# An attention-and-whitening kernel on one core: weight copies on GpSimd, and an image's last row point prepared in the strict order

## The chip, the cores and the metric

The kernel runs on one core of a Trainium2 chip. The core has five engines that run beside each other: TensorE (matrix multiplication, PE in the profile, with its weight loads as PEld), VectorE (DVE), ScalarE (ACT), GpSimd (POOL) and SyncE (SP, which here only issues DMAs). The metric is the device time of one execution in microseconds. The kernel before was timed in three runs: 761.77, 763.97 and 764.57 us, median 763.97.

## The reference

Input x has 4 images of 256 channels and 64 x 64 pixels, in float32. The first layer computes, for each pixel, 49 attention weights and uses them to average the pixel's dilated neighbourhood:

```python
k = conv(x, w1, 7x7, dilation 2, padding 6) + b1        # 256 -> 128 channels
k = conv(k, w2, 1x1) + b2                               # 128 -> 49
attn = softmax(k, axis=1)
shifts = stack([xp[:, :, 2*u:2*u+64, 2*v:2*v+64] for u in range(7) for v in range(7)])
x = einsum('bkchw,bkhw->bchw', shifts, attn)
```

The second layer whitens the result over the batch: the channels form 4 groups of 64, each group has its mean taken off and its 64 x 64 covariance computed over all images and pixels, five Newton steps give the inverse square root of the covariance, and that matrix is applied to each pixel, followed by a gain and a shift.

## The kernel before, in words

**The convolution.** The two convolutions are merged into one from 256 channels to 49 outputs. Because of the dilation of 2, the image splits into even and odd rows and columns. The 7 x 7 merged convolution is computed by evaluation at points, as in fast convolution: rows and columns each have seven points (0, 1, 2, 3, 4, 5 and INF, where INF is the leading coefficient). For one image and one *row point*, VectorE combines the image's rows (`row_eval`, tiles `rb`), then the columns of that for each column point (`col_ops`, tiles `xh`, through a scratch tile `ct`), TensorE multiplies by the weights of the pair of points (`conv_bank`, tiles `wr`, into the PSUM tiles `cv`), and ScalarE copies the sums to `pv` (line 541). The column points of a row point come in three groups, called banks: points 1, 2, 0, then 3, 4, INF, then 5. Bank 0 has 96 matrix instructions in the profile for a row point with two row taps, bank 1 has 80, and bank 2 has 32; the row point INF has half of each.

**Interpolation.** When a row point's three banks are in `pv`, VectorE turns its column points back into columns (`col_interp`, 22 operations, into the tiles `zz`). When an image has all of its row points, `row_interp` does the same over rows, into the logits `lgx`. At the end of an image this is cut in parts: `row_interp` part 0 follows row point 4, since it needs all row points but 5; row point 5's columns and the rest of the rows follow when its banks come.

**Order of row points.** Image 0 has a start of its own with a partly direct convolution. Image 1 uses the row points 0, 1, 2, 3, 4, 5, images 2 and 3 use INF, 0, 1, 2, 3, 4, 5 (`ROWS`, line 29, so `ROWS[-2]` is row point 4 and `ROWS[-1]` is 5). `conv_step(k, i)` runs bank i of the k-th row point and then prepares bank i of the next one (`prepare`, line 696): its weights, its rows if i is 0, and its columns. The preparation writes `xh` and `wr` tiles of which there is one for each bank, so it has to wait until TensorE has read the previous row point's bank i.

**Weights.** The weights of a pair of points are made once, the first time that a row point is used, and stored to DRAM (`weights`, line 361, store at 429); later images load them (line 375). Making them takes sums and scaled sums on VectorE (through `ct` from image 1 on), for the column points 0 and INF plain copies by ScalarE (lines 405, 406 and 415), and scaling by ScalarE (line 428). Row points 1, 2 and 3 are made for image 0. From image 1 on this happens for row points 0, 4 and 5 of image 1 and for INF of image 2. For 4, 5 and INF the row-combined weights are first brought into `rb[0]` by a DMA on SP's queue (line 384).

**The rest.** Beside an image's convolution runs the attention of the image before it: softmax, the copies of its terms to `zt` (line 906), their way through DRAM (`sd`) and back as a band matrix (`band`, loaded at line 947 and transposed by VectorE at 957), transposed blocks of x (`xb`, TensorE 975, ScalarE 983), the weighted sums y (TensorE 1004, ScalarE 1023), and the moments for the whitening (1036, 1044, 1057). The band tile is loaded again when the y matmuls that read it are done. GpSimd clears tiles and issues the loads of x and the spills of finished images (lines 130 and 1075). After the last image come the remaining sums, the Newton steps and the application.

**What sets the order.** A scheduler in the framework orders each engine's instructions from priorities (the place in the program, raised inside `tc.high_priority()`) and estimated times. TensorE's instructions keep the order of the program (`pe`). VectorE's may be moved, except where the kernel adds order by hand: `in_turn` (line 280) makes every sum behind `add`, `sub` and `madd` follow the last operation issued in the *strict order*, and inside `in_order()` each such operation becomes that last one, with high priority. The columns and rows at an image's end are in the strict order; preparations from image 1 on are not. Once ordered, an engine takes its instructions one after the other.

Of the kernel before, what the change touches and what calls it, by code (L numbers as in the profile page):

```python
# [23 lines left out]
INF = 6  # L24
# [4 lines left out]
ROWS = (INF, 0, 1, 2, 3, 4, 5)  # L29
# [3 lines left out]
def kernel(  # L33
# [29 lines left out]
    nc = tc.nc  # L63
# [25 lines left out]
    def taps(b):  # L89
        return (0,) if b == INF else (0, 1)  # L90
# [203 lines left out]
    @contextmanager  # L294
    def in_order():
        was = strict[0]
        strict[0] = True
        with tc.high_priority():
            yield
        strict[0] = was  # L300

    def add(o, a, b):
        return in_turn(TT(o, a, b, ALU.add))  # L303

    def sub(o, a, b):
        return in_turn(TT(o, a, b, ALU.subtract))  # L306

    def madd(o, a, f, b):

        return in_turn(STT(o, a, f, b, ALU.mult, ALU.add))  # L310
# [50 lines left out]
    def weights(b, br, i, mid=None):  # L361

        first = (br, i) not in made
        made.add((br, i))
        s0 = slot_of[BANKS[i][0]]
        ns = sum(len(taps(bc)) for bc in BANKS[i])  # L370
        nk = NSK * len(taps(br)) // 2
        wt = apool.tile([P, ns, NSK], F32, tag=f"wr{i}", name=f"wr_{b}_{br}_{i}")[:, :, :nk]
        w = {bc: wt[:, slot_of[bc] - s0 : slot_of[bc] - s0 + len(taps(bc))] for bc in BANKS[i]}
        if not first:
            nc.sync.dma_start(wt, gd[br][:, s0 : s0 + ns])
            return w

        if br == 0:
            g = [gr0[:, v] for v in range(KS)]
        elif br in kept:  # L380

            f = rb[0].rearrange("p q r c w -> p (q r c w)")[:, : KS * nk]
            if i == 0:
                nc.sync.dma_start(f, kept[br])
            f = f.rearrange("p (v a r k) -> p v a r k", v=KS, a=NCC, k=KT)
            g = [f[:, v] for v in range(KS)]
        else:
            g = [gbr[:, v] for v in range(KS)]
        g = [t.rearrange("p a r k -> p (a r k)") for t in g]

        e = ct.rearrange("p a b -> p (a b)") if b else store[4].rearrange("p c r w -> p (c r w)")
        e, o, e1 = (e[:, k * nk : (k + 1) * nk] for k in range(3))
        g0 = [g[KS - 1 - a] for a in range(4)]
        g1 = [g[KS - 5 - a] for a in range(3)]
        o0 = {bc: w[bc][:, 0] for bc in w}
        o1 = {bc: w[bc][:, 1] for bc in w if bc != INF}
        if i == 0:
            add(e, g0[0], g0[2])
            add(o, g0[1], g0[3])
            add(e1, g1[0], g1[2])  # L400
            add(o0[1], e, o)
            sub(o0[2], e, o)
            add(o1[1], e1, g1[1])
            sub(o1[2], e1, g1[1])
            nc.scalar.copy(o0[0], g0[0])
            nc.scalar.copy(o1[0], g1[0])
        elif i == 1:
            madd(e, g0[2], 4.0, g0[0])
            madd(o, g0[3], 4.0, g0[1])
            madd(e1, g1[2], 4.0, g1[0])  # L410
            madd(o0[3], o, 2.0, e)
            madd(o0[4], o, -2.0, e)
            madd(o1[3], g1[1], 2.0, e1)
            madd(o1[4], g1[1], -2.0, e1)
            nc.scalar.copy(o0[INF], g0[3])
        else:
            madd(o0[5], g0[0], 2.0, g0[1])
            madd(o1[5], g1[0], 4.0, g1[2])
            madd(o0[5], o0[5], 2.0, g0[2])
            if mid is not None:  # L420
                mid()
            madd(o1[5], g1[1], 2.0, o1[5])
            madd(o0[5], o0[5], 2.0, g0[3])
            add(o1[5], o1[5], o1[5])
        for bc in BANKS[i]:
            f = SCALE[bc] * (SCALE[br] if br not in kept else 1.0)
            if f != 1.0:
                nc.scalar.mul(w[bc], w[bc], f)
        nc.sync.dma_start(gd[br][:, s0 : s0 + ns], wt)
        return w  # L430

    def row_eval(b, br, rb=rb):

        for pr in range(2):
            xs = slots[2 * b + pr].rearrange("p c (q a) w -> p a q c w", a=4)
            r = [t[:, :, pr] for t in rb]
            if br == 1:
                add(r[0], xs[:, 0], xs[:, 2])
                add(r[1], xs[:, 1], xs[:, 3])
            elif br == 0:  # L440
                nc.scalar.copy(r[2], xs[:, 0])
            elif br == INF:
                nc.scalar.copy(r[1], xs[:, 3])
            X = [[xs[:, a, :, cc] for a in range(4)] for cc in range(NCC)]
            q = [[t[:, :, cc] for t in r] for cc in range(NCC)]
            for cc in range(NCC):
                if br == 3:
                    madd(q[cc][1], X[cc][2], 4.0, X[cc][0])
                    madd(q[cc][2], X[cc][3], 4.0, X[cc][1])
                elif br == 5:  # L450
                    madd(q[cc][2], X[cc][0], 2.0, X[cc][1])
            for a in (2, 3) if br == 5 else ():
                for cc in range(NCC):
                    madd(q[cc][2], q[cc][2], 2.0, X[cc][a])
        r = [t.rearrange("p q r c w -> p (q r c w)") for t in rb]
        if br == 1:
            add(r[2], r[0], r[1])
        elif br == 2:
            sub(r[0], r[0], r[1])
        elif br == 3:  # L460
            madd(r[0], r[2], 2.0, r[1])
        elif br == 4:
            madd(r[1], r[2], -2.0, r[1])
        return rb[{1: 2, 2: 0, 3: 0, 4: 1, 5: 2, 0: 2, INF: 1}[br]]
# [30 lines left out]
    def col_eval(src, i):  # L495
        for _ in col_ops(src, i):
            pass

    def both0(src, br, i):

        g = col_ops(src, i)
        next(g)
        nxt.update(weights(0, br, i, lambda: next(g)))
        for _ in g:
            pass
# [96 lines left out]
    def col_interp(b, br, part=None):  # L602
        at = slot[b, br]
        pt = {
            c: pv[:K2, at, i].rearrange("p q b -> p (q b)").rearrange(
                "p (q b two) -> p q b two", q=Q9, two=2
            )
            for i, c in enumerate(ORDER)
        }
        outs = phases(zz[:K2, br].rearrange("p q (w two) -> p q w two", two=2))  # L610
        cut = lambda t, k: t[:, :, k : k + Q8]
        if b > 0:

            t = pv[:K2, (at + 2) % NV, NP - 1].rearrange("p q b -> p (q b)")
        else:
            t = ct.rearrange("p a b -> p (a b)")[:K2, :PT]
        interpolate(
            pt, t.rearrange("p (q b two) -> p q b two", q=Q9, two=2), outs, cut, part
        )

        def end():
            ins = nc.scalar.copy(outs[3], cut(pt[5], 0))
            if br == INF:

                nc.gpsimd.memset(zz[:, INF, Q8], 0.0)
            return ins

        if part is None and b > 0 and br != ROWS[-2]:
            later.append(end)
        elif part != 0:  # L630
            end()
# [64 lines left out]
    def prepare(k, i):  # L696

        b, br = rows[k]
        w = weights(b, br, i)
        if i == 0:  # L700
            cur["x"] = row_eval(b, br)
        nxt.update(w)
        col_eval(cur["x"], i)

    def conv_step(k, i):
        w = {bc: nxt.pop(bc) for bc in BANKS[i]}
        b, br = rows[k]
        conv_bank(b, br, i, w)
        end = b > 0 and br == ROWS[-1]
        if end:  # L710

            with in_order():
                if i == len(BANKS) - 2:
                    col_interp(b, br, 0)
                elif i == len(BANKS) - 1:
                    col_interp(b, br, 1)
                    row_interp(b, 1)
        if k + 1 < len(rows):
            prepare(k + 1, i)
        if i == len(BANKS) - 1 and not end:  # L720
            last = br == ROWS[-2]
            with in_order() if last else nullcontext():
                col_interp(b, br)
                if last:
                    row_interp(b, 0)
# [24 lines left out]
    for i in three:  # L750
        nxt.update(weights(0, 1, i))
# [678 lines left out]
```

## Time and profile before

| | |
|---|---|
| median of three runs | 763.97 us |
| the profiled execution's own time | 761.8 us |
| its span, first to last instruction | 760.0 us |
| mean granted TensorE clock | 0.978 |
| busy: TensorE / VectorE / ScalarE / GpSimd | 698.6 / 643.0 / 342.8 / 33.7 us |
| ends of image 1, 2, 3 (row point 4's bank 2 to the last rows) | about 261 to 302, 419 to 458, 564 to 597 us |

A line of a timeline gives the start in us from the span's start, the length in us, the engine, the line of the kernel, the operation, out<-in with their shapes, and how many instructions are merged; a bracket at the end says how long the engine had stood idle before it and which instruction or DMA released it. The tables of stretches give for each engine its busy time and, in parentheses, its instructions. Starts on VectorE can be closer together than the lengths, since the end of an operation overlaps the start of the next. A matmul's end is modelled.

### The profile page before, as it was taken

How to read it: one execution, taken by the hardware profiler on the slowest of the kernel's cores; microseconds unless marked ns; L12 is line 12 of the kernel's file. 1: busy time of each engine (PE TensorE's matmuls, PEld its weight loads, DVE VectorE, ACT ScalarE, POOL GpSimd, SP SyncE). 2: the span in 40 equal slices, each digit the busy share in tenths (PEclk: the TensorE clock that was granted, in tenths of full speed). 3: DMA queues.
4: the chain of work that ended last, by engine and by line, in shares of the span. 5: the costliest groups of instructions: out<-in, count | busy, mean ns of one | idle time of the engine just before them, and what ended most of it. 6: DMA issues, size and time to landing. Idle time of an engine off the chain costs nothing.

```text
span 760.0 us, 18845 instructions
## 1 busy us (share of the span) xinstructions
PE 698.6 (92%) x7608; PEld 539.3 (71%) x7608; DVE 643.0 (85%) x1394; ACT 342.8 (45%) x980; POOL 33.7 (4%) x45
## 2 busy tenths in 40 slices
PE   6999999996999877999999977999999889998996
PEld 1459643376998766888998967998898668885322
DVE  3799899999999989999994999999979675545665
ACT  1414240255355726366545442745435473322464
POOL 0410000020000010002000100000000000000000
PEclk9999999999899989999999998999999999999999
DMA  8981120227163563246745731342532134363488
GB/s 323 254 293 72 60 86 0 87 98 233 33 220 120 198 216 88 80 141 217 226 137 184 233 105 47 126 111 91 165 90 79 50 98 140 117 232 136 191 357 338
DMA packets 62911, 115.39 MB, mean 152 GB/s; under 512 B 26295, under 2 KB 45416, under 8 KB 62056
## 3 DMA queue, kind: packets, MB, share of 16 engines
q1 hardware_dynamic: 59128, 95.31, 38.4%
q0 software_dynamic: 3696, 18.88, 7.2%
q8 instruction: 60, 0.98, 0.6%
q14 instruction: 27, 0.22, 0.1%
HBM read 66.18 MB, written 47.98 MB: 150 GB/s over the span
## 4 chain that ended last, share of the span: by engine, by line
DVE 44%; PE 41%; ACT 5%; DMA 4%; issue 4%; SPq 1%; DVEq 0%; ACTq 0%
PE cv L531 9%; PE y L1004 8%; PE acc L668 6%; DVE xh L310 6%; DVE pv L310 5%; DVE rb L310 4%; PE tp L1370 4%; DVE ct L310 3%; DVE band L957 3%; DVE ct L303 3%; DVE zz L310 3%; DVE pv L306 2%; PE tp L1036 2%; PE tp L975 2%; PE sig L1057 2%
## 5 line engine op out<-in xcount | busy, mean ns | idle before, releaser
L531 PE MATMUL cv<-xh,wr 128*49 128x128 f32 (+1 forms) x4576 | 268.8, 279 | 19.5 <-issue 7.3
L531 PEld LDWEIGHTS cv<-xh,wr 128*49 128x49 f32 x4576 | 260.6, 126 | 25.5 <-issue 18.0
L1004 PE MATMUL y<-band,xb 128*128 128x224 f32 (+2 forms) x640 | 151.2, 374 | 15.0 <-ACT xb L983 12.9
L1004 PEld LDWEIGHTS y<-band,xb 128*128 128x128 f32 x640 | 109.6, 193 | 36.4 <-ACT xb L983 16.0
L541 ACT COPY pv<-cv 113x486 f32<-113x486 f32 (+1 forms) x69 | 33.2, 483 | 101.8 <-PE cv L531 101.5
L1023 ACT ACTIVATE slot<-y,pivot 128x512 f32<-128x512 f32 x53 | 36.8, 741 | 62.1 <-PE y L1004 62.1
L310 DVE SCALAR_TENSOR_TENSOR pv<-pv 113x162 f32<-113x162 f32 x215 | 63.8, 318 | 0.5
L1044 ACT COPY yt<-tp 128x256 f32<-128x256 f32 x128 | 45.9, 379 | 36.3 <-PE tp L1036 35.2
L957 DVE STREAM_TRANSPOSE band<-band 128x960 f32<-128x960 f32 (+1 forms) x48 | 50.9, 1060 | 9.9 <-DMA band<-sd 9.9
L1036 PE MATMUL tp<-ident,slot 128*128 128x128 f32 x256 | 52.0, 299 | 4.4 <-ACT yt L1044 2.3
L975 PE MATMUL tp<-ident,slot 128*128 128x128 f32 x256 | 50.5, 300 | 4.6 <-ACT yt L1044 4.5
L1036 PEld LDWEIGHTS tp<-ident,slot 128*128 128x128 f32 x256 | 41.3, 205 | 13.3 <-issue 3.2
L975 PEld LDWEIGHTS tp<-ident,slot 128*128 128x128 f32 x256 | 40.4, 206 | 11.0 <-ACT yt L1044 6.0
L906 ACT COPY zt<-d 32x112 f32<-32x112 f32 (+2 forms) x156 | 45.0, 289 | 1.8
L860 ACT ACTIVATE d<-tp,mx 128x49 f32<-128x49 f32 x128 | 37.5, 335 | 14.0 <-DVE mx L855 10.7
L310 DVE SCALAR_TENSOR_TENSOR xh<-ct 128x512 f32<-128x512 f32 x46 | 30.3, 683 | 10.2 <-PE cv L531 10.2
L1057 PE MATMUL sig<-yt 128*64 128x65 f32 x1024 | 36.9, 225 | 0.0
L1057 PEld LDWEIGHTS sig<-yt 128*64 128x64 f32 x1024 | 32.5, 137 | 6.0 <-issue 4.5
L983 DVE COPY xb<-tp 128x256 f32<-128x256 f32 x41 | 16.4, 421 | 23.7 <-PE tp L975 23.7
L983 ACT COPY xb<-tp 128x256 f32<-128x256 f32 x87 | 30.4, 376 | 12.7 <-PE tp L975 12.0
L306 DVE TENSOR_TENSOR pv<-pv 113x162 f32<-113x162 f32 x112 | 34.6, 319 | 0.4
L668 PE MATMUL acc<-slot,tap 128*49 128x496 f32 (+3 forms) x168 | 34.6, 569 | 0.0
(221 smaller groups left out, 947.2 us busy)
## 6 DMA issues: line engine op xcount, KB each, us to landing
out_dram<-out SPq DMA_DIRECT2D x32, 512.0 KB, 3.4
sd<-zt SPq DMA_DIRECT2D x16, 896.0 KB, 4.2
slot<-in_x_dram POOLq DMA_DIRECT2D x12, 1024.0 KB, 9.2
band<-sd SPq DMA_DIRECT2D x128, 84.0 KB, 2.2
wr<-gd SPq DMA_DIRECT2D x15, 588.0 KB, 3.8
wr<-gd SPq DMA_DIRECT2D x15, 490.0 KB, 3.5
spill<-slot POOLq DMA_DIRECT2D x3, 2048.0 KB, 8.4
back<-spill SPq DMA_DIRECT2D x3, 2048.0 KB, 12.8
```

Of the source, the lines that this page charges most:

```text
L306: return in_turn(TT(o, a, b, ALU.subtract))
L310: return in_turn(STT(o, a, f, b, ALU.mult, ALU.add))
L531: nc.tensor.matmul(cv[h * HB : h * HB + KT, k, sr : sr + n, sc : sc + n], wv[:, sc, sr, cc], xh[bc][:, :n, h * NCC + cc, :n], start=(j == ...
L668: nc.tensor.matmul(ps[h * HB : h * HB + KT, :, w0:w1_], w[v][:, cc], xs[:, :, cc, w0 + d : w1_ + d], start=(j == 0), stop=(j == len(order) ...
L906: ins = nc.scalar.copy(o, i)
L957: nc.vector.transpose(f, f)
L975: nc.tensor.transpose(t[:, cc * P : (cc + 1) * P], xt[:, cc, CR * m : CR * (m + 1), bass.ds(pc, SW, 2)], ident,)
L983: (nc.vector.tensor_copy if tail else nc.scalar.copy)(xb, t[:, :C])
L1004: nc.tensor.matmul(ps[:, cc, q0 - half * HALF : q1 - half * HALF, :], xb[:, cc * P : (cc + 1) * P], rhs, start=(k == 0), stop=(k == len(PI ...
L1036: nc.tensor.transpose(t[:, cc * P : (cc + 1) * P], yt[:, cc, CR * i : CR * (i + 1), bass.ds(pc, SW, 2)], ident,)
L1044: nc.scalar.copy(yb.rearrange("p a g c -> p (a g) c")[:, :, :GW], t[:, :C].rearrange("p (e c) -> p e c", c=GW),)
L1057: nc.tensor.matmul(sig[g * GW : (g + 1) * GW, cc], yb[:, cc, g, :GW], yb[:, cc, g], start=(count[0] == 0 and cc == 0), stop=(count[0] == 4 ...
```

## The change

In `weights`, the plain copies for column points 0 and INF are made by ScalarE for image 0 and by GpSimd for the images after it. In `conv_step`, where the row point under way is the last but one of an image after the first, and the bank is not the first, the preparation of the next row point (row point 5) is issued inside `in_order()`. So its VectorE sums join the strict order ahead of the columns of row point 4 and of the rows that follow in the program, and all that it issues, its DMAs and copies too, has high priority.

```diff
@@ weights
+        same = nc.scalar.copy if b == 0 else nc.gpsimd.tensor_copy
         if i == 0:
...
-            nc.scalar.copy(o0[0], g0[0])
-            nc.scalar.copy(o1[0], g1[0])
+            same(o0[0], g0[0])
+            same(o1[0], g1[0])
         elif i == 1:
...
-            nc.scalar.copy(o0[INF], g0[3])
+            same(o0[INF], g0[3])
@@ conv_step
         if k + 1 < len(rows):
-            prepare(k + 1, i)
+            with in_order() if b > 0 and br == ROWS[-2] and i > 0 else nullcontext():
+                prepare(k + 1, i)
         if i == len(BANKS) - 1 and not end:
             last = br == ROWS[-2]
             with in_order() if last else nullcontext():
                 col_interp(b, br)
                 if last:
                     row_interp(b, 0)
```

## The prediction

> **What bounds the kernel now.** I read the page first. Its busy table has TensorE and VectorE both near full, ScalarE under half, GpSimd nearly empty, so one total settles nothing and the stretches around the change must be read one by one.
>
> ```profile
> PE 698.6 (92%) x7608; PEld 539.3 (71%) x7608; DVE 643.0 (85%) x1394; ACT 342.8 (45%) x980; POOL 33.7 (4%) x45
> DVE 44%; PE 41%; ACT 5%; DMA 4%; issue 4%; SPq 1%; DVEq 0%; ACTq 0%
> ```
>
> Second, the table of stretches (columns: stretch, length, busy us and count of TensorE, its weight loads, VectorE, ScalarE, GpSimd, then granted clock, DMA share, GB/s).
>
> ```profile
> 252.00:264.00 12.00, 9.66 (x134) 8.37 (x136) 11.86 (x33) 9.30 (x27) 0.57 (x1) 1.00 0.66 244
> 264.00:286.00 22.00, 17.68 (x200) 16.11 (x198) 18.48 (x36) 6.29 (x17) 3.38 (x2) 0.84 0.65 216
> 286.00:298.00 12.00, 10.49 (x118) 8.82 (x114) 12.00 (x40) 10.07 (x22) 0.00 (x0) 1.00 0.28 58
> 440.00:461.00 21.00, 12.32 (x151) 10.09 (x151) 20.62 (x43) 8.43 (x19) 0.00 (x0) 0.91 0.31 85
> ```
>
> Around the ends of images VectorE is the full engine and TensorE has the holes. The one large VectorE hole before 350 us is in the second row. Third, the timelines of that hole; ScalarE, TensorE and VectorE in turn:
>
> ```profile
> 271.39 0.35 ACT L983 COPY xb<-tp 128x256 f32<-128x256 f32 x1
> 276.85 0.27 ACT L405 COPY wr<-rb 128x98 f32<-128x98 f32 x1 [5.10 <-DMA rb<-gi]
> 277.03 0.27 ACT L406 COPY wr<-rb 128x98 f32<-128x98 f32 x1
> 277.20 0.36 ACT L983 COPY xb<-tp 128x256 f32<-128x256 f32 x1
> ...
> 277.62 1.17 PE L1004 MATMUL y<-band,xb 128*128 128x96 f32 x4 [4.32 <-ACT xb L983]
> ...
> 282.94 1.18 DVE L957 STREAM_TRANSPOSE band<-band 128x960 f32<-128x960 f32 x1 [3.52 <-DMA band<-sd]
> ```
>
> A weight copy sits on ScalarE until its input lands. The xb copy behind it is late, the y matmuls that need xb are late, the band they read is released late, and VectorE stands 3.52 us at the band's transpose. In the chain of waits the DMA that fed the copy (rb<-gi) left at 270.01, when the last weight operation of row point 5 but one had read the same buffer.
>
> Fourth, image 2's end, VectorE and TensorE:
>
> ```profile
> 419.42 0.65 DVE L310 SCALAR_TENSOR_TENSOR xh<-ct 128x512 f32<-128x512 f32 x1
> 420.20 0.33 DVE L303 TENSOR_TENSOR pv<-pv 113x162 f32<-113x162 f32 x1
> 420.57 0.33 DVE L306 TENSOR_TENSOR pv<-pv 113x162 f32<-113x162 f32 x1
> ...
> 421.54 0.68 DVE L310 SCALAR_TENSOR_TENSOR xh<-rb 128x512 f32<-128x512 f32 x1
> ...
> 427.69 0.75 DVE L303 TENSOR_TENSOR ct<-zz 113x576 f32<-113x576 f32 x1
> ...
> 414.55 11.64 PE L531 MATMUL cv<-xh,wr 128*49 128x128 f32 x206
> ```
>
> Here columns (pv) start while the third bank of row point 4 is still on TensorE, and the preparation of row point 5 (xh<-rb) is slipped between them.
>
> **What the Trainium skill says.** "Perfetto Trace Analysis", section on the Tensor Engine instruction, says ScalarE, VectorE and GpSimd are strict FIFOs; the 5.10 us above with xb directly behind agree. "GPSIMD Engine Reference", section 3.1, gives about 1.8 cycles per element at 1.2 GHz as the best rate; the trace's two 128x64 copies by GpSimd take 0.41 us together, so 196 elements come to an estimated 0.44 us (0.24 + 132 x 1.5 ns). Its section 1 says GpSimd shares its SBUF interface with VectorE's two-input operations; no GpSimd copy here overlaps VectorE work, so no run shows it yet. "Perfetto Trace Analysis", Optimizing Scalar/DVE Operations, says the write acknowledgement overlaps the next instruction; the trace agrees: independent pv operations are 0.24 us apart (423.45 to 423.69), chained ones 0.36 to 0.37 (420.20 to 420.57). Chaining costs 0.12 each.
>
> **The change, part by part.**
>
> *Copies.* Twelve leave ScalarE (three for each of image 1's row points 0, 4, 5 and image 2's INF): nine of about 0.36 and three of 0.27, 4.2 us. ScalarE is 45% busy, so the busy time itself is worth nothing; what hides it is ScalarE's own waiting for matmuls (9.5 us between 252 and 300). On GpSimd they come to 9 x 0.44 + 3 x 0.29 (98 elements) = 4.8 us, bounded by 3 (0.25 each) and 12 (1.0 each, VectorE holding the port). VectorE could lose as much as they overlap, at most some 2 us; I take 0. The waits matter more. Behind the copy that waits 5.10 us stand xb and the y store; freed, the y matmuls start near 272.9 instead of 277.62, 4.7 us earlier. On GpSimd the copy's neighbours are the spill at 258.96, slot loads at 268.07 and 269.76 and a memset at 331.58. If it stands ahead of the loads they leave about 5 us later; they land 8.4 to 12.5 us after issue and are read at 288.28, so at least 6 us of slack cover that. The result is wanted only at 297.06. At 98.8 and 230 to 254 us GpSimd's queue is free until the DMA at 145.93 and the spill at 258.96. The weight store on SP now waits for GpSimd too, 0.1 us later than for ScalarE. I take 0 for each.
>
> *Strict order, image 1.* The first half (7 weight operations, ct, two xh; its scales on ScalarE and store on SP move with it) can start at 255.3 as now, because ct is busy until then. The second half (6 weight operations and three xh) writes buffers that bank 2 of row point 4 still reads: TensorE starts it at 261.49, 32 matmuls x 56.6 ns end at 263.3. Today VectorE fills the time up to there with 16 of the 22 column operations of row point 4 (254.47 to 260.47), 16 x 0.238 = 3.8 us. In strict order these queue behind the second half. So VectorE's 11.4 us of work from 252.60 to 264.0 shrink to 7.6; with 0.2 for chaining and the 1.09 us transpose now at 264.08 pulled in, it ends at 261.5 and stands 1.8 us. From 263.3 on: today's 264.08 to 285.88 is 21.8 us; less the 3.52 us hole, which goes because y and band come early (rb<-gi too, at about 266), less the transpose 1.09, plus 3.8 of column operations, plus 1.4 for some twelve chained operations that no longer have another between them: 22.4, ending at 285.7 against 285.88. The freed ScalarE wait is paid back by VectorE: -0.2 us. xh5 is ready at about 267 instead of 285.3 and TensorE ends bank 2 near 281.5 instead of 287.7, but the next matmuls wait for VectorE's xh all the same (3.55 us at 303.48 today). What is late next is VectorE.
>
> *Strict order, image 2.* Weights are only loaded. Their DMAs wait for the same matmuls as before (419.25 on SP) and the band loads queued behind are issued from 430.43, so 0. On VectorE the second half waits for bank 2: b1 starts at 414.72, 112 matmuls x 56.5 ns end at 421.05. VectorE ends xh4 at 420.07 and stands 1.0. Then three chained xh 2.05, then columns: today 420.20 to 427.69 is 7.49, less three xh 1.8, plus three exposed chainings 0.36, 6.05. Rows begin at 429.15, not 427.69: +1.5. VectorE is full to 460 and TensorE stands 7.34 us until 460.68 for its last xh, then is 38.7 of 39 us busy, so it carries to the end.
>
> *Strict order, image 3.* The same: bank 2 ends at 565.5, 2.05 + 6.05 give 573.6 against 572.07: +1.5. It reaches TensorE through the zz copy at 591.47, which waits for VectorE with xb behind it.
>
> Sum: -0.2 + 1.5 + 1.5 = +2.8 us on the profiled execution's 761.8 (span 760.0, 1.8 around it), 764.6. That execution is 2.2 below the median 763.97; the same sum there gives 766.8 us, +0.37%. Less than 0.5% (3.8 us) is about what a measurement of this kernel can tell from no change.
>
> **Rivals.** A (likeliest, 40%): as summed, 764.5 to 769.
>
> B, faster (30%): the ScalarE wait is the true bound. For it: the chain of waits runs through rb<-gi, ScalarE and TensorE from 270 to 299. Against: VectorE is busy for all of 286 to 299.5. If the order finds other cover for VectorE's 1.8 us, the 4.7 us of the y matmuls stay; image 2's +1.5 is met if at image 3 xb comes ahead of the zz copy (TensorE's wait of 1.6 at 592.11 goes): 759.3.
>
> C, slower (20%): the strict order's hold on VectorE at image 1 with nothing won. If the band stays late (its release or its DMA), the 3.52 us hole remains and the 960-wide transpose cannot fill the gap: 2.9 idle + 1.4 chaining, with 3.0 at the later ends 7.3, giving 771.3. It decides once more than about 2 us of the hole remain; for it speaks that VectorE's other transposes also wait for band (3.24 at 409.39).
>
> D (10%): other work takes the moved places, 764.
>
> **How the numbers follow.** A puts 28 within 0.5% and 12 slower (its upper end passes 767.8); B 24 faster and 6 within; C 20 slower; D 10 within. Faster 0.24, same 0.44, slower 0.32. A tenth below and a tenth above are cut in B and C: 758.5 to 772.5.
>
> **What would show it.** Right: no ScalarE wait on rb<-gi; y matmuls near 273; no 3.5 us hole at the band transpose but one of about 2 us before the second half at 263; xh<-rb three in a row ahead of pv at images 2 and 3, with the start of rows 1.5 us later after the end of bank 1. Wrong: columns of row point 4 still running before 263, VectorE reaching image 1's last columns clearly before 285, or GpSimd copies that TensorE waits for.

## The result, and the profile after

The kernel after takes 767.27 us, median of five runs (765.94 to 768.35); the kernel before, run beside it, takes 763.87 us (761.77 to 764.57). The ratio is 1.0049 with a 95% interval of 1.003 to 1.0069: slower by about 0.5%, or 3.4 us between the medians. The profiled execution of after took 765.94 us with a span of 764.2, against 761.8 and 760.0 before. The experiments below ran in three groups, each beside the kernel before; single executions scattered more there than here (before itself from 761.4 to 777.1 us), so they are read by their ratios, which leave disturbed executions out.

The page's busy table and its chain of work, after:

```profile
PE 698.5 (91%) x7608; PEld 539.6 (71%) x7608; DVE 645.8 (85%) x1394; ACT 340.5 (45%) x968; POOL 55.1 (7%) x57
DVE 43%; PE 43%; DMA 5%; issue 4%; ACT 3%; SPq 1%; DVEq 0%; ACTq 0%
```

Twelve copies have gone from ScalarE to GpSimd (980 to 968, and 45 to 57). GpSimd's busy time rose by 21.4 us, not by 4.8; two of the twelve copies make up most of it. No total says where 4 us were lost. For that I set the starts of ScalarE's 69 copies of sums to `pv`, which have one fixed order in both kernels, against each other. After runs 0.3 us behind before at 249 us, 4.0 behind at 331, still 4.0 at 421, 5.9 at 506, 5.9 at 566, and 4.1 at 585. The last of the 69, right behind, is 7.3 late, for it has changed its place among ScalarE's other work; TensorE's matmuls, which all keep one order too, are 4.1 behind at 604 and stay there to the end. So image 1's end costs 3.7, the stretch of image 2's end 1.9, and in the stretch of image 3's end 1.8 is given back. How much of the last is the change's own is taken up below.

VectorE's timeline at image 1's end, after (a bracket says how long VectorE had stood before the operation and for what):

```profile
260.12 0.84 DVE L961 STREAM_TRANSPOSE band<-band 128x640 f32<-128x640 f32 x1
263.98 0.63 DVE L310 SCALAR_TENSOR_TENSOR wr<-rb 128x196 f32<-128x196 f32 x2 [3.02 <-issue]
...
266.89 1.18 DVE L961 STREAM_TRANSPOSE band<-band 128x960 f32<-128x960 f32 x1 [0.58 <-DMA band<-sd]
267.99 1.38 DVE L310 SCALAR_TENSOR_TENSOR xh<-xh,rb 128x512 f32<-128x512 f32 x2
269.28 0.32 DVE L303 TENSOR_TENSOR pv<-pv 113x162 f32<-113x162 f32 x1
...
282.28 1.18 DVE L961 STREAM_TRANSPOSE band<-band 128x960 f32<-128x960 f32 x1 [1.33 <-DMA band<-sd]
...
289.47 0.76 DVE L303 TENSOR_TENSOR zz<-ct,zz 113x576 f32<-113x576 f32 x1
290.14 0.32 DVE L303 TENSOR_TENSOR pv<-pv 113x162 f32<-113x162 f32 x1
```

The last line is row point 5's columns, which began at 285.88 before: 4.26 us later. The stand in front of bank 2's weights is 3.02 us, not 1.8, because the 960-wide transpose that was to fill it waits for its own DMA and comes after. The bracket names no releaser for the stand; in all four kernels that have the strict order at image 1 it ends 2.05 us after TensorE began bank 2 (261.93 to 263.98 here), about the length of that bank's 32 matmuls. And the hole of before at the later band transpose, 3.52 us, has not gone; 1.33 of it is still there. Idle time in this stretch is 3.02 + 0.58 + 1.33 = 4.93 us against 3.52, which is 1.41 more. The other 2.46 us is VectorE's own occupation: I summed, for each kind of operation between 252.6 and row point 5's columns, the time from its start to the next start, less idle time. The counts are the same in both kernels.

| operations | before, us | after, us |
|---|---|---|
| pv (19) | 4.45 | 5.67 |
| zz, 576 wide (11) | 7.36 | 8.01 |
| xh, 512 wide (7) | 4.22 | 4.52 |
| the rest | 13.73 | 14.02 |
| sum | 29.76 | 32.22 |

Packed behind each other, dependent operations start 0.36 us apart (269.28 to 269.64) where before another operation stood between them. Seven of the pv operations do. Four others, from 272.52 to 273.46, start 0.30 to 0.33 us apart without being chained: GpSimd makes two of the weight copies beside them (273.07 to 273.66). In the strict order alone (below), where ScalarE makes those copies, the pv operations there are 0.24 apart, and the extra occupation of the stretch is 2.11 us and not 2.46. With the later start of the stretch (0.39 us) the three terms give the 4.26.

ScalarE in the same place, after:

```profile
274.33 0.32 ACT L624 COPY zz<-pv 113x144 f32<-113x144 f32 x1 [2.24 <-DVE pv L310]
274.55 0.37 ACT L987 COPY xb<-tp 128x256 f32<-128x256 f32 x1
```

and TensorE:

```profile
274.97 0.69 PE L1008 MATMUL y<-band,xb 128*128 128x96 f32 x4 [1.23 <-ACT xb L987]
...
299.85 4.84 PE L533 MATMUL cv<-xh,wr 128*49 128x128 f32 x48 [8.76 <-DVE xh L303]
```

ScalarE no longer waits for rb<-gi, but a copy of `zz` now waits 2.24 us for the columns that the strict order put off, with the same xb copy behind it. The y matmuls still start 2.65 us earlier than before. It is no use to TensorE: until 299.85 it stands 8.76 us for VectorE's xh. Before, the same matmuls began at 297.06 without a stand; the next ones, which stood 3.55 us until 303.48, begin at 307.48 after.

### The profile page after: what moved, and what is told of

The parts are those of the page before. It is cut to its first block, busy times and chain, and to the rows that moved or that the text cites. A ratio compares the mean times of both kernels' runs of the same rounds, so it can differ in the third digit from the quotient of the medians.

```text
span 764.2 us, 18870 instructions
## 1 busy us (share of the span) xinstructions
PE 698.5 (91%) x7608; PEld 539.6 (71%) x7608; DVE 645.8 (85%) x1394; ACT 340.5 (45%) x968; POOL 55.1 (7%) x57
## 4 chain that ended last, share of the span: by engine, by line
DVE 43%; PE 43%; DMA 5%; issue 4%; ACT 3%; SPq 1%; DVEq 0%; ACTq 0%
PE cv L533 10%; PE y L1008 8%; PE acc L670 6%; DVE xh L310 5%; DVE pv L310 4%; DVE rb L310 4%; PE tp L1374 4%; DVE zz L310 3%; DVE band L961 3%; DVE ct L310 3%; DMA band<-sd 3%; DVE ct L303 3%; PE tp L1040 2%; PE tp L979 2%; DVE pv L306 2%
```

## Experiments: one part at a time

The first group takes the change apart. The copies alone:

```diff
-            with in_order() if b > 0 and br == ROWS[-2] and i > 0 else nullcontext():
+            with nullcontext():
                 prepare(k + 1, i)
```

> Only the twelve copies move to GpSimd; the preparation keeps its old order. Theory T1 (the copies win, the strict order costs): ScalarE's 5.10 us wait for the row weights is gone, the four y matmuls start near 273 instead of 277.6, VectorE's 3.52 us hole before the band transpose closes, and VectorE's order is the old one, so no new hole before 263: about 3.5 us less than before, 760.4 (between 759 and 762). Theory T2 (the copies cost, by VectorE and GpSimd sharing a port or by late weights): no gain, 764 to 768.

Measured: ratio 0.9992 (0.9977 to 1.0007), no gain that can be told from nothing. The first theory failed. The number is the second's, but the profile gives another reason than the two that it names. VectorE's timeline:

```profile
285.43 1.18 DVE L961 STREAM_TRANSPOSE band<-band 128x960 f32<-128x960 f32 x1 [2.64 <-DMA band<-sd]
```

and the piece in front of it in the chain of work:

```profile
277.53 7.78 DMA band<-sd
```

ScalarE's wait has gone, and the hole of VectorE is there all the same: the band's transfer takes 7.78 us.

The strict order alone:

```diff
-        same = nc.scalar.copy if b == 0 else nc.gpsimd.tensor_copy
+        same = nc.scalar.copy
```

> Only the order changes; ScalarE makes all copies as before. T1: the changed kernel plus what the copies win, that is 767.3 + about 3.5 = 770 to 771, since ScalarE's wait for the row weights is back in some size (the DMA leaves 4 us earlier now, so it may be only 1 to 4 us). T2: 764 or a little less.

Measured: 1.0024 (1.0009 to 1.004), some 1.8 us, which is between the times of the two theories. About half of the 0.0049 of the whole change is there without any copy on GpSimd.

The copies with the strict order at image 1 only (`b == 1` in place of `b > 0`), and at images 2 and 3 only (`b > 1`):

> Copies on GpSimd, strict order at the end of image 1 alone. T1, by the offsets read from the two traces (+4.0 us after image 1's end, +1.9 at image 2's, -1.6 at image 3's): 763.9 + 4.0 = 767.9. T2 (the ends of images 2 and 3 are what costs): 760 to 764.

> Copies on GpSimd, strict order at the ends of images 2 and 3 alone. T1: the copies' -3.5, then +1.9 and -1.6: 760.7. VectorE stands 1.0 us before the three xh operations of image 2 and rows begin 1.5 to 2 us later relative to bank 1's end; at image 3 the xb copy runs ahead of the zz copy on ScalarE. T2: 767 or more.

Measured: 1.0049 (1.0035 to 1.0063) and 0.9996 (0.9983 to 1.0009). So image 1's part alone costs what the whole change costs: 1.0049 - 0.9992 = 0.0057 more than the copies alone, 4.4 us. The later ends come to 0.0004, 0.3 us, together: neither the 760.7 of the one theory, which counted on copies that win 3.5, nor the 767 of the other. A cost at image 2 and a gain of the same size at image 3 would add up to that.

## Experiments: why the copies win nothing

In the kernel before, the four band loads behind VectorE's hole were issued here (SyncE's queue), long before the y matmuls at 277.62 that I had taken for their release:

```profile
272.35 2.17 SPq L947 DMA_DIRECT2D band<-sd  x4
```

Taken by themselves (the uses of `sd` in the window 271 to 276 us), they landed like this:

```profile
DMA to landing us min/median/max: 8.9/9.4/9.7
```

They are 84 KB each. Two loads of 1 MB into slot 0 (image 2's odd rows, issued by GpSimd from 268.07 to 271.5) are in flight until about 281. The next two runs leave those loads out, from before and from the copies alone (their output is then not the reference's):

```diff
-            load_x(k, nxt_k, nc.gpsimd)
+            if k == 0:
+                slots[nxt_k] = store[0]
+            else:
+                load_x(k, nxt_k, nc.gpsimd)
```

> The kernel before, with the two 1 MB loads of image 2's odd rows into slot 0 left out (the odd rows of image 2 are then computed from what slot 0 held, so its output is not the reference's; every instruction of the engines stays). Theory of contention: in the profile of before the transfer rb<-gi lands after 6.82 us because the two slot loads (268 to 281 us) are in flight beside it; without them it lands in 3 to 4 us, ScalarE's wait at image 1's end shrinks by about 3 us, and the kernel takes about 761 us (ratio 0.995 to 0.997). Rival, the small transfer is slow on its own account: it still takes 6 us or more, and the time is that of before within 1 us.

> The copies on GpSimd alone, without the strict order, and with the two slot loads left out as in the kernel before without these loads. Theory of contention: with the ScalarE wait gone, the 960-wide band's transfer lands in 2 to 4 us and not in 7.8, VectorE's hole of 2.6 us in front of its transpose goes, and the kernel takes 3 to 4 us less than copies alone: ratio to before about 0.995. If the ScalarE wait and the band's transfer are both only lengthened by these loads, this kernel and the kernel before without the loads come out within 1.5 us of one another. Rival: the band's transfer stays at 6 us or more without the loads, and the time is that of the copies alone (ratio 0.999).

Measured: 0.998 (0.9961 to 0.9998) and 0.997 (0.995 to 0.999). The table of stretches, 268 to 282 us (after the stretch and its length: busy us and count of TensorE, its weight loads, VectorE, ScalarE, GpSimd; then granted clock, DMA share, GB/s), first of before:

```profile
268.00:282.00 14.00, 9.68 (x68) 8.15 (x66) 11.42 (x20) 4.92 (x12) 3.38 (x2) 0.80 0.76 236
```

and then of before without the loads:

```profile
268.00:282.00 14.00, 11.76 (x108) 10.08 (x106) 14.00 (x25) 5.59 (x13) 0.00 (x0) 0.88 0.30 89
```

Its band loads' landing:

```profile
DMA to landing us min/median/max: 2.2/2.3/2.5
```

Its timelines of ScalarE (the weight copy that waits) and of VectorE (the transpose):

```profile
275.16 0.27 ACT L405 COPY wr<-rb 128x98 f32<-128x98 f32 x1 [2.33 <-DMA rb<-gi]
```

```profile
280.41 1.17 DVE L957 STREAM_TRANSPOSE band<-band 128x960 f32<-128x960 f32 x1
```

This kernel still makes the copies on ScalarE, ScalarE still waits for rb<-gi (which lands after 4.0 us and not 6.8), and VectorE has no hole at all: 14.00 us busy of 14.00. (The granted clock differs too, 0.80 and 0.88, so TensorE's part of the difference is not all due to the loads.) The hole was never ScalarE's. It belongs to a transfer that shares the DMA engines with 2 MB of loads: 9.4 us to land beside them, 2.3 without. "DMA: Bandwidth & Descriptors" in the Trainium skill, section Queues, rings and completion order, says that each DMA engine takes turns between the queues it has work for, a whole packet at a time; I infer that a small transfer beside a large one waits at every turn; the two landings agree with that, though no run here shows the turns.

The sizes agree less well than the mechanism. Leaving the loads out gains 1.5 and 2.3 us (0.002 and 0.003 of 765) where I expected about 3 and 4. In the profile of before without the loads the `pv` copies are 2.8 us early at 331 us, but only 1.2 early at 506: part of it is lost again at image 2's end.

Could the loads be made harmless? They wait for the 2 MB spill of the same slot. Spilling in halves lets the first load start early:

```diff
-            nc.gpsimd.dma_start(spill[k], slots[k].rearrange("p a r w -> p (a r w)"))
+            for cc in range(NCC):
+                nc.gpsimd.dma_start(
+                    spill[k][:, cc * SH * W : (cc + 1) * SH * W],
+                    slots[k][:, cc].rearrange("p r w -> p (r w)"),
+                )
```

> The kernel before, with each 2 MB copy of a slot to its spill made as two transfers of 1 MB, so that the first load into the slot need only wait for the first half. ScalarE's order around 288 us changes by a few copies with it. Theory of contention: the spill lands after 8.4 us in the profile of before and the loads start then; with halves the first load starts about 4 us sooner, all of it is done near 277 and not 281, and rb<-gi and the 960-wide band land 2 to 4 us sooner: 1 to 2.5 us faster, ratio 0.997 to 0.9985 (leaving the loads out gave 0.998). Rival: the DMA engines are full from 260 to 281 us, so the same 4 MB end at the same time, ratio 0.9995 to 1.001.

> The copies on GpSimd alone with the spills in halves. Theory of contention: the 960-wide band lands in 3 to 5 us in place of 7.8, VectorE's hole in front of its transpose shrinks from 2.6 to under 1 us, ratio to before 0.9965 to 0.998 (without the loads: 0.997). Rival: DMA engines full, ratio 0.999 as with the copies alone.

Measured: 1.0023 (1.0 to 1.0046) and 0.9988 (0.9968 to 1.0007). No gain; before came out slower if anything (its interval begins at 1.0). In before with halves VectorE's hole does shrink to 0.81 us, but the chain shows what pays for it:

```profile
269.97 8.51 DMA rb<-gi
```

That is 6.82 in before: the lateness has moved onto the other small transfer. The loads do land sooner (at 279.0 us, before at 282.3), but the DMA engines are busy for 0.89 of the time from 260 to 281 us in both kernels, as the rival had it. Which of the two small ones is late changes, the time does not improve. ScalarE's order near 288 us changes with this edit too, so the 0.2% of split_before is not put down to the DMAs alone.

## Experiments: is image 1's cost a late transfer too?

The whole change without the two slot loads:

> The whole change, with the two slot loads of image 2's odd rows left out (its output is then not the reference's). If the strict order's cost at image 1's end (4 us) is VectorE's own work put in a row, it stays without the loads: the hole of 1.3 us in front of the band's transpose near 282 us goes, the stand of 3.0 us at 264 stays, and the kernel takes 1 to 2 us less than the change, ratio to before 1.001 to 1.003, that is 3 to 4.5 us above the copies alone without the loads (0.997). Rival, the cost at image 1 is a late transfer behind the loads: the kernel comes to within 1 us of the copies alone without the loads, ratio 0.996 to 0.998.

Measured: 1.0046 (1.0023 to 1.007), that is 0.0076 (5.8 us) above the copies alone without the loads, which ran in another group. VectorE at image 1's end in this run:

```profile
265.48 0.63 DVE L310 SCALAR_TENSOR_TENSOR wr<-rb 128x196 f32<-128x196 f32 x2 [3.04 <-issue]
...
268.67 1.18 DVE L961 STREAM_TRANSPOSE band<-band 128x960 f32<-128x960 f32 x1 [0.86 <-DMA band<-sd]
```

The hole near 282 is gone, as expected, and the stand of 3 us in front of bank 2's weights is untouched. The rival, that a late transfer is what the strict order pays for, has fallen: the order costs its 4 to 6 us with the loads and without. But the 1 to 2 us that I expected from the vanished hole don't show in the time; the profile has 1.1 of them (image 1's end at +2.6 in place of +3.7). By the profiles the cost is VectorE held back until TensorE has done bank 2 (3.0 us with nothing allowed ahead), and chained columns afterwards; no run took one of these away by itself.

## Experiments: image 3's gain, and a better kernel

The strict order at image 3 only, with the copies:

```diff
-            with in_order() if b > 0 and br == ROWS[-2] and i > 0 else nullcontext():
+            with in_order() if b == 3 and br == ROWS[-2] and i > 0 else nullcontext():
```

> The change with the strict order at image 3's end only (copies from image 1 on as in the change). By the evictions' offsets image 3's end alone gains 1.7 us (xb ahead of the zz copy on ScalarE), images 1 and 2 keep their order, and the copies are worth 0 to -0.6: about 762.0 to 763.5 where before has 764.5 (ratio 0.997 to 0.9985). If image 3's gain was only the place that image 2's delay left behind, ratio 0.999 to 1.000.

Measured: 0.9966 (0.995 to 0.9981), faster than before by 2.6 us and faster than after. The same with the spills in halves:

> Copies on GpSimd, strict order at image 3's end only, and the spills in halves. If the gain of the halves (0.002) and that of the copies with image 3's strict order (0.0034) add up: ratio 0.994 to 0.996. If the halves bring nothing: 0.9966. If image 3's gain was noise of its chip: 0.998 to 0.999.

Measured: 0.9965 (0.9944 to 0.9985). The halves add nothing, and the gain over before is there in a second group of runs. Against the copies alone with the spills in halves (0.9988, same group) it is 0.0023, 1.8 us, though these two intervals overlap.

The offsets of all runs against before's profile, over the three stretches named in the result (pv copies at 249 to 331, 421 to 506 and 566 to 585 us of before), in us. The last column follows TensorE instead, from 571 us to its matmul at 603.62 us of before:

| kernel | image 1 | image 2 | image 3 | image 3, TensorE |
|---|---|---|---|---|
| after | +3.7 | +1.9 | -1.75 | -1.8 |
| strict order alone | +3.8 | +1.3 | -1.75 | -1.8 |
| copies, strict at 1 | +4.6 | +1.0 | 0.0 | -1.0 |
| after without the loads | +2.6 | +1.3 | -1.74 | -1.8 |
| copies, strict at 2 and 3 | -1.6 | +1.3 | -1.74 | -1.8 |
| copies, strict at 3 | -1.8 | +1.3 | -1.75 | -1.8 |
| the same, spills in halves | +0.2 | +1.3 | -1.75 | -1.8 |
| copies alone | +1.3 | +1.2 | 0.0 | -1.0 |
| copies, row point 4's zz on GpSimd | -1.7 | +1.8 | -0.1 | -1.1 |
| copies alone without the loads | -2.4 | 0.0 | 0.0 | -0.6 |
| copies alone, spills in halves | -0.6 | +1.5 | 0.0 | -1.0 |
| before without the loads | -3.0 | +1.6 | 0.0 | -1.0 |
| before, spills in halves | +3.7 | +0.2 | 0.0 | -1.0 |

The column of image 1 must not be read too closely. Copies alone, strict at 2 and 3, and strict at 3 order every engine alike up to there, and yet show +1.3, -1.6 and -1.8. In each profile the granted TensorE clock falls to half for stretches of 3.4 to 10.2 us, at other places each time, and copies alone has one where TensorE is full. First copies alone, then strict at 2 and 3 at the same place (columns as above; the clock is the third number from the end):

```profile
257.10:260.50 3.40, 3.40 (x9) 2.08 (x7) 3.40 (x15) 0.00 (x0) 0.00 (x0) 0.50 0.26 73
257.10:260.50 3.40, 3.40 (x46) 2.81 (x44) 3.40 (x15) 1.76 (x4) 0.09 (x1) 1.00 0.37 97
```

Its offset grows from 1.2 us at 249 to 3.4 at 265, the other's from 1.2 to 1.5. The two kernels with the copies and the spills in halves have such a stretch at 255 and at 260 us, and theirs grow by 2.0 and 2.4. What the order costs at image 1 therefore rests on the times (4.4 and 5.8 us above), not on this column.

Image 3's column looks clear: all six kernels that have the strict order there gain 1.75, the seven others nothing. But the pv copy that it ends with has changed places: before, ScalarE makes it behind a copy of lgx (line 650) that waits 1.68 us for VectorE, and with the strict order it comes first. TensorE's own column has 1.8 in the six and 0.6 to 1.1 in the seven others, which have no strict order there. All thirteen share something else: before's profile alone has a stretch at half clock there:

```profile
593.90:597.30 3.40, 3.40 (x14) 3.11 (x15) 2.89 (x6) 2.87 (x7) 0.54 (x3) 0.50 0.01 2
```

So 0.7 to 1.2 us are left for the order. How they come, first from before (ScalarE's zz copy of row point 5 with xb behind it, then TensorE):

```profile
591.47 0.32 ACT L622 COPY zz<-pv 113x144 f32<-113x144 f32 x1 [2.53 <-DVE pv L310]
591.69 0.36 ACT L983 COPY xb<-tp 128x256 f32<-128x256 f32 x1
...
592.11 0.69 PE L1004 MATMUL y<-band,xb 128*128 128x96 f32 x4 [1.60 <-ACT xb L983]
```

and from after:

```profile
596.51 0.37 ACT L987 COPY xb<-tp 128x256 f32<-128x256 f32 x1 [0.90 <-PE tp L979]
597.65 1.35 ACT L1027 ACTIVATE slot<-y,pivot 128x512 f32<-128x512 f32 x2 [0.78 <-PE y L1008]
598.93 0.33 ACT L624 COPY zz<-pv 113x144 f32<-113x144 f32 x1
```

After, xb and the y stores stand ahead of the zz copy. TensorE's 1.60 us for that xb is no longer in its timeline; against it stand about 0.7 and 0.6 us that it loses to other copies, around 586.8 and 598.8 us of before.

An attempt to get this without the order, moving a zz copy to GpSimd:

```diff
-            ins = nc.scalar.copy(outs[3], cut(pt[5], 0))
+            same = nc.gpsimd.tensor_copy if b > 0 and br == ROWS[-2] else nc.scalar.copy
+            ins = same(outs[3], cut(pt[5], 0))
```

> The copies on GpSimd alone, and the copy of zz at each image's last row point (images 1 to 3, L622 of the kernel before) on GpSimd too, no strict order. Theory: what image 3's end gains in the change is that xb no longer waits behind the zz copy on ScalarE; moved to GpSimd the copy holds nothing, so image 3's end gains about 1.6 us without the strict order, images 1 and 2 gain 0 to 0.5: ratio 0.996 to 0.998. Rival: the zz copy on GpSimd ends later and holds the rows behind it on VectorE, ratio 1.000 to 1.002.

Measured: 1.0007 (0.9984 to 1.003). My edit moved row point 4's copy. The one that holds xb at image 3 is row point 5's, and in this run's profile it is still on ScalarE at 593.25. So the run says nothing against the explanation, and moving the right copy was not tried.

Image 2 is not clear from the table, since seven of the nine kernels without the strict order there show +1.0 to +1.8, as those with it do. VectorE's own line says a little more. After, image 2's end:

```profile
425.07 0.68 DVE L310 SCALAR_TENSOR_TENSOR xh<-rb 128x512 f32<-128x512 f32 x1
425.79 1.42 DVE L310 SCALAR_TENSOR_TENSOR xh<-xh,rb 128x512 f32<-128x512 f32 x2
433.16 0.75 DVE L303 TENSOR_TENSOR ct<-zz 113x576 f32<-113x576 f32 x1
```

Less the 4.01 us by which the kernel is behind there, rows begin at 429.15, 1.46 later than before's 427.69. All four kernels with the strict order at image 2 give 1.44 to 1.46; the nine others give 0.0 to 1.6, without a pattern that I can name. In times, strict order at images 2 and 3 (0.9996) and at 3 alone (0.9966) differ by 0.003, some 2.3 us for image 2, but these are from two groups and their intervals nearly meet. A cost of the order at image 2 is likely, and not shown.

## Why the prediction was right, and where it was not

The forecast of 766.8 us against 767.27 measured is close; +2.8 against the profiled execution's +4.1 is less so. The terms behind it are not close: that the sum came out is luck, for two errors of opposite sign met, one at image 1 and one at image 3.

- **Image 1, -0.2 said, +3.7 found.** The step that failed is "less the 3.52 us hole, which goes because y and band come early". The hole had nothing to do with ScalarE's wait or the y matmuls' start. The band loads had left at 272.35, and their landing took 9.4 us beside the slot loads, which stay when the weight copies move. After, 1.33 us of the hole remain, and 0.58 is new in front of the transpose before it.
- **The stand before bank 2.** 1.8 said, 3.02 found. The failing step is "the 1.09 us transpose now at 264.08 pulled in": that transpose waits for a DMA until 266.89. Without it my own sum gives 2.9.
- **Chaining.** 1.4 + 0.2 said, 2.46 found as extra occupation, with the same number of operations; 2.11 of it is there in the strict order alone. The price of 0.12 was right; I counted about a dozen exposures, but pv alone has seven of them (0.84 of its 1.22 us), and rows and xh have more. About 0.3 of the rest is pv operations beside GpSimd's copies, which the prediction put at nothing.
- **Rival C** had the mechanism at image 1, "2.9 idle + 1.4 chaining" if the band stays late: 4.3 against 3.7 to 4.3 found, though less of the hole remained than the 2 us at which it was to decide. It missed on image 3.
- **Image 2, +1.5 said.** Rows begin 1.46 us later, by the mechanism named, three xh in a row. The stretch in the profile has +1.9, though kernels without the order at image 2 have 0.0 to +1.8 there.
- **Image 3, +1.5 said, -1.8 found, of which 0.7 to 1.2 is the order's.** Rows do begin 1.58 us later (in all six kernels). The step that failed is the last: "It reaches TensorE through the zz copy". The zz copy lost its place ahead of xb, as rival B had it, and TensorE lost nothing by the delay.
- **Copies.** No wait on rb<-gi, as said. y matmuls near 272.9 said, 274.97 found; the step left out is that ScalarE has a second copy in the same place, the zz copy, whose input the strict order delays. Their whole worth alone was 0.6 us, and that is within the interval of nothing.
- **GpSimd's copies**, 0.44 us estimated for 128x196. After has

```profile
97.25 13.82 POOL L407 COPY wr<-lgx 128x196 f32<-128x196 f32 x1 [52.98 <-ACT lgx L788]
111.01 0.45 POOL L408 COPY wr<-lgx 128x196 f32<-128x196 f32 x1
...
229.54 0.81 POOL L408 COPY wr<-rb 128x196 f32<-128x196 f32 x1
247.83 0.36 POOL L407 COPY wr<-rb 128x196 f32<-128x196 f32 x1 [16.73 <-ACT rb L445]
250.18 2.99 POOL L417 COPY wr<-rb 128x196 f32<-128x196 f32 x1 [1.59 <-PE tp L1040]
```

Seven of the nine lie between 0.36 and 0.81, within the bounds of 0.25 to 1.0; the two others are told of below. For VectorE beside them the prediction took 0, and by the trace it loses a little (below). The pv copies around them are in place to 0.3 us until 249 us, so there the loss stayed small.

What stays open: why the strict order alone (1.0024) costs less than with the copies at image 1 (1.0049, same group), when the copies alone cost nothing. The intervals don't overlap much, and no line of the profile names it.

## What to carry to other kernels

A wait named in the profile for a DMA is either a late issue or a slow landing, and these call for different changes: look at when the transfer was issued, and at what else was in flight, before the delay is charged to the engine whose work seems to precede it. Forcing a stream ahead in program order pays twice on a full in-order engine: it stands where the stream's input isn't ready and nothing may pass, and work that had hidden the gaps between dependent operations is packed into chains of its own. And test each place of a change that touches several: here the same edit cost 4 us at one and gave something back at another, and the kernel with the good place alone (0.9966) beats both. Before a gain at one place is read from two profiles, see what that place does in kernels without the change: here they moved by 0.6 to 1.1 us too, with the granted clock.

## What the runs showed of the hardware

In before, four transfers of 84 KB landed 8.9 to 9.7 us after issue beside two 1 MB loads; in the three kernels without these loads they took 2.1 to 3.1 us. Splitting the spill only chose which small one was late (rb<-gi went from 6.82 to 8.51 us while the band's wait fell from 3.52 to 0.81).

GpSimd and VectorE hinder each other, which before could not show. Beside a GpSimd copy three of VectorE's row sums take 0.83 us in place of 0.68. Two of them after, and the same sums before (time in ns):

```profile
L310 DVE SCALAR_TENSOR_TENSOR rb<-rb,slot x2: 828/829/830, 229.3 to 230.1; 128x512 f32<-128x512 f32 x2
L310 DVE SCALAR_TENSOR_TENSOR rb<-rb,slot x4: 678/680/681, 229.5 to 231.3; 128x512 f32<-128x512 f32 x4
```

Two GpSimd copies of 128x196, 0.36 to 0.81 us elsewhere, are shown as 13.82 us and 2.99 us. While they last VectorE's operations follow each other without a pause; its first pauses end at 110.89 and 252.99, and the copies end at 111.07 and 253.17, both 0.18 us later. All ten kernels with these copies on GpSimd have the first at 13.81 to 13.82 us, and nine have the other at 2.99 to 3.27, each ending 0.2 us after VectorE's first pause; in the tenth, strict at 3 with the spills in halves, the other took 0.55. So these copies seem to wait for a gap in VectorE's work. Not every copy beside a busy VectorE does, as the 0.81 shows, and no run tells what decides it. The profile shows no engine that waited for either of the two.
